# Last-visit chunk products of a gather-sum kernel: one float32 product becomes two float32r products

## The chip, the cores and the metric

The kernel runs on one NeuronCore of a Trainium2 chip. The metric is the device time of one execution in microseconds (us). The engines are TensorE (PE; PEld is its weight load), VectorE (DVE), ScalarE (ACT), GpSimd (POOL) and SyncE (SP, which issues DMAs).

## What is computed

The reference sums the features of 206,250 edges by their source node, puts the sums through a three-layer network with the node's own row, and normalises the result:

```python
edge_aggr = jnp.zeros((n, 128)).at[src].add(edge_attr_128)
combined = concatenate([x, edge_aggr, global_expand], axis=-1) @ W_c + b_c
h = softplus(combined @ W1 + b1)
h = softplus(h @ W2 + b2)
return layernorm(x + (h @ W3 + b3))
```

There are n = 6,250 nodes, and each row has 128 float32 values.

## The kernel before

The nodes are cut into 32 buckets of 196 (`BL`). The edge rows are read, sorted within a column of 122 by TensorE (line 1156), copied out of PSUM by ScalarE (line 1168) and scattered by 846 indirect DMAs of GpSimd (line 1185) into *rooms* of their bucket in the DRAM tensor `rows_by`. Once a stretch of a room is sure to be full, SP loads up to eight chunks of 128 rows back (a *load*, tile `chunks`, `AHEAD` = 6 of them in turn). A *visit* is a set of such chunks of one pair of buckets; a *unit* is at most four chunks of a load (`HALF`).

For each unit `match` (line 974) lets VectorE write one-hot tiles `hot` of 128 x 196 per chunk (line 985: is the row's place in its bucket equal to the column?), and `product` (line 993) multiplies each chunk's 128 x 128 rows with its one-hot tile on TensorE and accumulates in the PSUM tile `part` (line 1008). When a visit is complete, `add` (line 1017) lets VectorE add `part` into `sums_t` (line 1031). The last visits of all rooms have `col == NC`: they can be loaded only when every scatter has landed.

What is left of these steps when the sorting is over is the list `rest`, and `node_layers` (line 1337) weaves it into the network. There are 13 node tiles of up to 512 nodes. For a tile TensorE forms z of layer 1 (lines 1347 and 1348, the second needs the tile's sums), ScalarE runs three activations (1358, 1359, 1364), VectorE makes h (1372), TensorE forms z of layer 2 (1351), ScalarE and VectorE follow again, TensorE makes the last product (1386), and VectorE adds the node rows and takes the statistics (1394, 1397, 1401). `norm` (line 1405) runs for groups of three node tiles: a few small operations on VectorE and ScalarE give the factors `rs`, and then GpSimd normalises 12 blocks of 128 nodes (line 1428) and issues three output DMAs (line 1431). In the last two groups other engines do it or share it. GpSimd also adds the bias b3 to all node rows beforehand (line 1447).

The order on TensorE, VectorE, ScalarE and SP is the order in which the code is written out (`manual_schedule`), and GpSimd keeps the order of the program too. In `rest` the match of a unit is written four units ahead of its product (`AT_END`). An engine takes its instructions strictly in that order, so that one that waits holds up all behind it.

Of the kernel before, what the change touches and what calls it, by code (L numbers as in the profile page):

```python
# [6 lines left out]

F32 = mybir.dt.float32
BF16 = mybir.dt.bfloat16
F16 = mybir.dt.float16  # L10
I32 = mybir.dt.int32
# [3 lines left out]
ALU = mybir.AluOpType  # L15
# [3 lines left out]
P = 128  # L19

BL = 196
# [36 lines left out]
HALF = 4  # L58
# [15 lines left out]
SPAN = 48  # L74

SUMS = 2

ROWS = 4
BANKS = 3
# [63 lines left out]
def kernel(  # L143
# [21 lines left out]
    nc = tc.nc  # L165
    N, D = n_nodes, x.shape[2]
# [5 lines left out]
    NC = 2 * TB  # L172
# [67 lines left out]

    plain = const.tile(list(plain_in.shape), F32, name="plain")
    half = const.tile(list(half_in.shape), BF16, name="half")

# [11 lines left out]
    ident_h, wide_h = (of_half[n] for n in ("ident", "wide"))  # L255
    ones = const.tile([P, P], F32, name="ones")
    ones_h = const.tile([P, P], BF16, name="ones_h")
    zero_c = const.tile([P, ROW - W], F32, name="zero_c")
    sums_t = const.tile([P, NB * BL], F32, name="sums_t")
    most_of = const.tile([KB, 6 * G], F32, name="most_of")  # L260
    many_i = const.tile([1, 1], I32, name="many_i")
    c_bias = const.tile([P, 1], F32, name="c_bias")
    weights_sb = const.tile(list(weights_in.shape), F32, name="weights_sb")
# [13 lines left out]
    rows_by = dram.tile([ROWS_ALL, ROW], F32, name="rows_by")  # L277
    totals = dram.tile([N + 2, D], F32, name="totals")

    put = {"todo": []}  # L280

    def rows_dma(out, in_):
        for _ in range(2):
# [22 lines left out]
    hots = ctx.enter_context(tc.tile_pool(name="hots", bufs=6))  # L306
# [8 lines left out]
    with ExitStack() as phase:  # L315
# [15 lines left out]
        pair_i = src_i[:PN]  # L331
        pair_block = keep.tile([PN, NC], BF16, name="pair_block")
        pair_low = pair_i.bitcast(F32)
# [113 lines left out]
        def positions(g):  # L447
# [18 lines left out]
            def opened2():  # L466
                slot_of[g] = per.tile([P, 2 * B_MAX], F32, name="slot", bufs=3)
                pair_of[g] = per.tile([P, B_MAX], I32, name="pair", bufs=3)

            def opened():  # L470
                if sets:
                    if not split:
                        opened2()
                    own["odd"] = per.tile([KB, 2, Q_MAX], BF16, name="odd", bufs=1)
                    own["evens"] = per.tile([KB, Q_MAX], BF16, name="evens", bufs=1)
                    own["alone"] = per.tile([KB, Q_MAX], BF16, name="alone", bufs=1)
                    late, deep = ("_late", G - GAP) if split else ("", 1)
# [403 lines left out]
        def sum_steps():  # L881

            def form(item):
                of, b, c = item
                return (0, b) if not of else (THREE, 0) if of == THREE else (1 + (c >= CUT), 0)

            loads, units_of, in_visit = [], [], {}
            for v, (col, order, b0, b1, all_of) in enumerate(visits()):
# [18 lines left out]
                for of in mine:  # L907
                    if not of:
                        continue
                    n = -(-len(of) // HALF)  # L910
# [5 lines left out]
            for n, (j, _, _) in enumerate(units_of):  # L916
                last_unit[j] = n
            base_of = {v: min(bs) for v, bs in in_visit.items()}
            chunks, hots_of, parts_of, met, begun = {}, {}, {}, {}, set()
            awaits = [0]  # L920

            def load(j):
# [43 lines left out]
            def place_in(j, q):  # L966
                all_of = loads[j][3]
                of, _, c = all_of[q]
                if of in (0, THREE):
                    return q  # L970
                mixed = [x for x, item in enumerate(all_of) if form(item) == form(all_of[q])]
                return mixed[0] + 2 * (c - all_of[mixed[0]][2]) + of - 1

            def match(n):
                j, a, e = units_of[n]
                hot = hots.tile([P, HALF, BL], F32, name="hot")
                hots_of[n] = hot
                q = a
                while q < e:
                    lo = hi = place_in(j, q)  # L980
                    step, m = 1, 1
                    while q + m < e and place_in(j, q + m) > hi and (m == 1 or place_in(j, q + m) == hi + step):
                        step, hi = place_in(j, q + m) - hi, place_in(j, q + m)
                        m += 1
                    nc.vector.tensor_tensor(  # L985
                        hot[:, q - a:q - a + m],
                        chunks[j][:, lo:hi + 1:step, D:W].to_broadcast([P, m, BL]),
                        iota_ps.unsqueeze(1).to_broadcast([P, m, BL]), op=ALU.is_equal)
                    q += m
# [3 lines left out]
            def product(n):  # L993
                j, a, e = units_of[n]
                v, col, order, all_of = loads[j]
                t, hot = chunks[j], hots_of.pop(n)
                if v not in parts_of:
                    while len(pending) > SUMS - 1:
                        add()
                    parts_of[v] = ps.tile([P, 2, BL], F32, name="part", bufs=SUMS)  # L1000
                    met[v] = []
                part = parts_of[v]
                for q in range(a, e):
                    b = all_of[q][1]
                    first = b not in met[v]
                    met[v].append(b)
                    last = met[v].count(b) == in_visit[v].count(b)
                    nc.tensor.matmul(part[:, b - base_of[v], :], t[:, place_in(j, q), :D], hot[:, q - a],  # L1008
                                     start=first, stop=last)
                if n == last_unit[j]:  # L1010
                    del chunks[j]
                if len(met[v]) == len(in_visit[v]):
                    pending.append((v, order, col, n))
                if pending and n >= pending[0][3] + BEHIND:
                    add()

            def add():
                v, order, col, _ = pending.pop(0)
                part = parts_of.pop(v)
                got = sorted(set(met.pop(v)))  # L1020
                new = [b for b in got if b not in begun]
                begun.update(new)
                for bs, to in ((new, True), ([b for b in got if b not in new], False)):
                    if not bs:
                        continue
                    here = sums_t[:, bs[0] * BL:(bs[-1] + 1) * BL]
                    of = part[:, bs[0] - base_of[v]:bs[-1] - base_of[v] + 1].rearrange("p b n -> p (b n)")
                    if to:
                        nc.vector.tensor_copy(here, of)
                    else:  # L1030
                        nc.vector.tensor_add(here, here, of)  # L1031
                if col == NC:
                    summed["to"] = (NB if got[-1] == NB - 1 else got[-1]) * BL
# [3 lines left out]
            for n, (j, a, e) in enumerate(units_of):  # L1037
                while opened < j or (opened + 1 < len(loads) and opened + 1 <= j + AHEAD - 1
                                     and opened + 1 - AHEAD in freed):
                    opened += 1  # L1040
                    ready = FIRST + SCATTER * (loads[opened][1] // 2) + LAG
                    load_at[opened] = max(ready, freed.get(opened - AHEAD, 0.0))
                    found.append((load_at[opened], len(found), lambda j=opened: load(j)))
                    if opened < AHEAD:
                        freed.setdefault(opened - AHEAD, 0.0)
                ahead = AT_END if at > ends[-1] else TOGETHER
                match_at.append(max(load_at[j] + MATCHED, product_at[n - ahead] if n >= ahead else 0.0))
                product_at[n] = max(at, match_at[n] + MULTIPLIED)
                found.append((match_at[n], len(found), lambda n=n: match(n)))
                found.append((product_at[n], len(found), lambda n=n: product(n)))  # L1050
                at = product_at[n] + (e - a) * RATE
                if n == last_unit[j]:
                    freed[j] = product_at[n]
# [143 lines left out]
        with tc.manual_schedule(engines={ET.PE, ET.DVE, ET.Activation, ET.SP}):  # L1197
            by_part = src.rearrange("(p t) -> p t", p=P)

            def src_cols(a, b):  # L1200
# [7 lines left out]
                name=nc.get_next_instruction_name(), act_func_set_id=TABLES))  # L1208
# [89 lines left out]
            for g in range(G):  # L1298
# [9 lines left out]
                if NODES[0] <= g < NODES[1]:  # L1308
                    upto = len(nodes)
                    part = nodes[held:upto]  # L1310
# [6 lines left out]
            todo = fill_rows()  # L1317
# [13 lines left out]

    ahead = ctx.enter_context(tc.tile_pool(name="ahead", bufs=1))
    work = ctx.enter_context(tc.tile_pool(name="work", bufs=1))

    many = nc.values_load(many_i[:1, :1], min_val=0, max_val=6 * G * KB)

# [148 lines left out]
    with tc.If(many > 0):  # L1485
# [4 lines left out]
        for a in range(0, N + 2, P):  # L1490
            b = min(N + 2, a + P)
            nc.sync.dma_start(totals[a:b, :], zeros[:b - a])
        with tc.For_i(0, runs // every, 1) as i:
            rows = slow.tile([P, W], F32, name="slow_rows")
            part = slow.tile([P, 1], I32, name="slow_part")
# [8 lines left out]
            v = nc.vector  # L1504
# [13 lines left out]
            for n, by in enumerate((wide_h, ident_h)):  # L1518
# [8 lines left out]
                             start=True, stop=True)  # L1527
# [78 lines left out]
```

## Time and profile before

| | |
|---|---|
| three runs | 1298.19, 1300.34, 1302.69 us, median 1300.34 us |
| the profiled execution | 1298.19 us, its span 1296.3 us |
| mean granted TensorE clock | 0.966 |
| TensorE, VectorE, ScalarE, GpSimd busy | 1167.5, 1073.0, 1063.7, 877.4 us |

The span is what lies between the first and the last instruction; 1.89 us of the execution lie around it. In a row of a group, "busy" is the time that the group occupied the engine, and the mean is the length of one instruction; on TensorE instructions overlap, so that the pace of a stream is read from the distance of its starts. "idle before" names what ended the engine's wait. A float32 product stands as two MATMUL records, since it goes through TensorE in two passes, each with its own weight load.

### The profile page before, as it was taken

What the parts mean: (1) busy time and instruction counts of PE and PEld (TensorE: products, weight loads), DVE (VectorE), ACT (ScalarE), POOL (GpSimd) and SP (SyncE); (2) the same over time, 40 slices, a digit from 0 to 9 for tenths busy, and PEclk for the clock granted to TensorE, in tenths of its full rate; (3) what the DMA queues carried; (4) which work ended last, traced back from release to release, by engine and by line L of the source; (5) the groups of instructions that cost most, each with busy time, mean ns of one, the idle gap of its engine ahead of it and who ended that gap; (6) DMA issues with size and microseconds to landing.
All of it is one profiled execution on the core that took longest, in us unless ns stands there. A gap on an engine that the chain in (4) does not pass through costs nothing.

```text
span 1296.3 us, 26649 instructions
## 1 busy us (share of the span) xinstructions
PE 1167.5 (90%) x8617; PEld 1106.5 (85%) x8617; DVE 1073.0 (83%) x2403; ACT 1063.7 (82%) x2484; POOL 877.4 (68%) x915
## 2 busy tenths in 40 slices
PE   5767898878999898999899999999999999999893
PEld 4667788877998898998799999999999999898762
DVE  7968987998899988899878887799877766687784
ACT  5998998899987898987999999998999999504353
POOL 2777777777775677776777777777777777730334
PEclk9988998989999899999999999999999999999996
DMA  6789998899999999997989999999999999874421
GB/s 228 245 292 369 335 342 291 303 319 377 335 364 299 354 381 355 355 312 244 313 291 303 331 333 318 355 313 320 326 354 328 370 332 355 280 210 143 143 76 53
DMA packets 228719, 387.21 MB, mean 299 GB/s; under 512 B 27914, under 2 KB 139218, under 8 KB 228190
## 3 DMA queue, kind: packets, MB, share of 16 engines
q1 hardware_dynamic: 184831, 265.91, 63.1%
q0 software_dynamic: 41328, 115.65, 23.1%
q10 hardware_dynamic: 2415, 3.87, 0.8%
q8 instruction: 72, 1.18, 0.4%
q14 instruction: 73, 0.60, 0.1%
HBM read 242.49 MB, written 147.41 MB: 301 GB/s over the span
## 4 chain that ended last, share of the span: by engine, by line
PE 47%; DVE 18%; DMA 11%; ACT 8%; issue 8%; POOL 7%; SPq 0%; ACTq 0%; DVEq 0%; POOLq 0%
PE part L1008 27%; PE sorted L1156 14%; DMA rows_by<-pairs,pair 8%; POOL rows_by L1185 7%; ACT pairs L1168 5%; DVE hot L985 4%; DMA chunks<-rows_by 2%; ACT sort_hot L1143 2%; DVE sort_hot L1136 2%; DVE pair_ib L493 2%; DVE past L722 2%; DVE sums_t L1031 1%; DVE slot L571 1%; PE small L552 1%; PE small L554 1%
## 5 line engine op out<-in xcount | busy, mean ns | idle before, releaser
L1185 POOL DMA_INDIRECT rows_by<-pairs,pair x846 | 825.0, 975 | 305.2 <-issue 208.0
L1008 PE MATMUL part<-hot,chunks 128*128 128x196 f32 x3516 | 674.6, 335 | 12.8 <-DVE sums_t L1031 9.9
L1168 ACT COPY pairs<-sorted 64x387 f32<-64x387 f32 (+2 forms) x1144 | 542.6, 474 | 82.3 <-PE sorted L1156 62.7
L1008 PEld LDWEIGHTS part<-hot,chunks 128*128 128x128 f32 x3516 | 581.1, 193 | 22.0 <-DVE sums_t L1031 11.3
L1156 PE MATMUL sorted<-rows,sort_hot 122*128 122x129 f32 x3384 | 495.8, 287 | 44.4 <-ACT pairs L1168 35.4
L1156 PEld LDWEIGHTS sorted<-rows,sort_hot 122*128 122x128 f32 x3384 | 453.1, 198 | 55.9 <-ACT pairs L1168 52.8
L985 DVE TENSOR_TENSOR hot<-chunks,both_ps 128x784 f32<-128x784 f32 (+3 forms) x541 | 428.1, 810 | 5.4 <-DMA chunks<-rows_by 5.0
L1143 ACT ACTIVATE sort_hot<-plain,slot 122x128 f32<-122x128 f32 x846 | 278.3, 391 | 12.6 <-DVE slot L571 6.7
L1031 DVE TENSOR_TENSOR sums_t<-sums_t,part 128x392 f32<-128x392 f32 (+1 forms) x262 | 143.5, 548 | 118.0 <-PE part L1008 117.4
L1145 ACT ACTIVATE sort_hot<-sort_hot,ones 122x384 f32<-122x384 f32 (+2 forms) x286 | 174.6, 611 | 9.3
L1136 DVE TENSOR_TENSOR sort_hot<-slot,both_ps 122x384 f32<-122x384 f32 (+2 forms) x286 | 154.5, 541 | 3.2 <-PE sorted L1156 3.0
L493 DVE TENSOR_TENSOR pair_ib<-pair_block,both_ps 122x512 bf16<-122x512 bf16 (+2 forms) x157 | 103.5, 664 | 0.3
L1428 POOL TENSOR_SCALAR y<-y,mv,rs 128x128 f32<-128x128 f32 x40 | 31.1, 785 | 98.8 <-issue 69.5
L571 DVE TENSOR_REDUCE slot<-small 122x16 f32<-122x512 f32 (+2 forms) x109 | 72.8, 668 | 15.1 <-PE small L554 15.0
L1358 ACT ACTIVATE away<-sorted,z_bias 128x512 f32<-128x512 f32 (+2 forms) x13 | 8.5, 656 | 71.7 <-DMA chunks<-rows_by 47.1
L552 PE MATMUL small<-pair_ib,half 122*122 122x512 bf16 (+2 forms) x109 | 43.1, 395 | 10.1 <-DVE slot L571 9.8
L737 PEld LDWEIGHTS <-past 128*128 128x128 f16 x424 | 24.8, 99 | 18.7 <-DVE past L722 13.5
L722 DVE TENSOR_TENSOR past<-both_ps,starts 128x512 f16<-128x512 f32 (+1 forms) x61 | 39.9, 666 | 0.2
L737 PE MATMUL small<-jump,past 128*128 128x56 f16 (+3 forms) x424 | 29.2, 190 | 11.9 <-DVE past L722 8.8
L554 PEld LDWEIGHTS <-starts_h 128*122 128x122 bf16 x236 | 25.0, 147 | 12.2 <-issue 7.8
L722 DVE TENSOR_TENSOR past<-both_ps,starts_late 128x512 f16<-128x512 f32 (+2 forms) x49 | 32.3, 660 | 0.0
L504 PE MATMUL small<-ones_h,pair_ib 122*128 122x48 bf16 x423 | 18.0, 188 | 14.8 <-DVE pair_ib L493 14.7
(163 smaller groups left out, 523.6 us busy)
## 6 DMA issues: line engine op xcount, KB each, us to landing
rows<-in_edge SPq DMA_DIRECT2D x105, 1032.0 KB
chunks<-rows_by SPq DMA_DIRECT2D x362, 136.0 KB
chunks<-rows_by SPq DMA_DIRECT2D x203, 204.0 KB
chunks<-rows_by SPq DMA_DIRECT2D x75, 272.0 KB
rows_by<-pairs,pair POOLq DMA_INDIRECT x846
rows_by<-fill SPq DMA_DIRECT2D x21, 544.0 KB
rows_by<-fill SPq DMA_DIRECT2D x14, 816.0 KB
chunks<-rows_by SPq DMA_DIRECT2D x13, 408.0 KB
```

Of the source, the lines that this page charges most:

```text
L493: nc.vector.tensor_tensor(ib, pair_block[:, cols].unsqueeze(2).to_broadcast([PN, n, SB]), iota_ps[:PN, :SB].unsqueeze(1).to_broadcast([PN, ...
L571: nc.vector.tensor_reduce(to, of, axis=mybir.AxisListType.X, op=ALU.max)
L722: nc.vector.tensor_tensor(past[:, :, a:b], twice_ps[:KB].unsqueeze(1).unsqueeze(1).to_broadcast([KB, 2, b - a, P // 2]), own["starts"][:, ...
L985: nc.vector.tensor_tensor(hot[:, q - a:q - a + m], chunks[j][:, lo:hi + 1:step, D:W].to_broadcast([P, m, BL]), iota_ps.unsqueeze(1).to_bro ...
L1008: nc.tensor.matmul(part[:, b - base_of[v], :], t[:, place_in(j, q), :D], hot[:, q - a], start=first, stop=last)
L1031: nc.vector.tensor_add(here, here, of)
L1136: nc.vector.tensor_tensor(hot[:PN, :m], slot[:PN, at:at + 2 * m - 1:2].unsqueeze(2).to_broadcast([PN, m, P]), slot_ps[:PN].unsqueeze(1).to ...
L1143: nc.scalar.activation(hot[:PN, j], by_slot[:PN], AF.Abs, bias=slot[:PN, at:at + 1], scale=-1.0)
L1145: nc.scalar.activation(hot[:PN, :m], hot[:PN, :m], AF.Relu, bias=ones[:PN, :1], scale=-1.0)
L1156: nc.tensor.matmul(out[:, j, :], hot[:PN, j], rows_at[col // LOAD_COLS][:PN, col % LOAD_COLS, :], start=True, stop=True)
L1168: nc.scalar.copy(sets_at[i][64 * n:64 * n + 64, lo:lo + m, h, :W], out[64 * h:64 * h + 64, :m, :])
L1185: s = nc.gpsimd.indirect_dma_start(out=dst, out_offset=bass.IndirectOffsetOnAxis(ap=at, axis=0), in_=rows[:, j].rearrange("p a b -> p (a b ...
```

## The change

For units of the last visits (`fine`), each run of chunks in `match` is split before the one-hot is made: ScalarE copies the rows into a float32r tile `high` (which rounds them), GpSimd subtracts it from the rows and writes the remainder as the float32r tile `low`, and the one-hot tile is float32r as well. In `product` each chunk then has two products, `high` and `low`, in place of one of float32. The two new tiles have six buffers each. Other units keep the float32 product; their one-hot is the same bits read as float32.

```diff
+HALVES_AHEAD = 6
...
-                hot = hots.tile([P, HALF, BL], F32, name="hot")
+                hot = hots.tile([P, HALF, BL], F32R, name="hot")
+                fine = loads[j][1] == NC
+                if fine:
+                    part_of[n] = [late["pool"].tile([P, HALF, D], F32R, name=f"{name}_of", bufs=HALVES_AHEAD)
+                                  for name in ("high", "low")]
+                else:
+                    hot = hot.bitcast(F32)
...
+                    if fine:
+                        whole = chunks[j][:, lo:hi + 1:step, :D]
+                        high, low = (part[:, q - a:q - a + m] for part in part_of[n])
+                        nc.scalar.copy(high, whole)
+                        nc.gpsimd.tensor_tensor(low, whole, high.bitcast(F32), op=ALU.subtract)
                     nc.vector.tensor_tensor(
                         hot[:, q - a:q - a + m],
...
-                    nc.tensor.matmul(part[:, b - base_of[v], :], t[:, place_in(j, q), :D], hot[:, q - a],
-                                     start=first, stop=last)
+                    rows = [p[:, q - a] for p in part_of[n]] if n in part_of else [t[:, place_in(j, q), :D]]
+                    for k, of in enumerate(rows):
+                        nc.tensor.matmul(part[:, b - base_of[v], :], of, hot[:, q - a],
+                                         start=first and k == 0, stop=last and k == len(rows) - 1)
```

By the order of the program 196 chunks in 56 units are changed, with 66 copies on ScalarE and 66 subtractions on GpSimd: 32 of each over four chunks (128x512), 32 over two (128x256), one over three and one over one. VectorE's and SP's order is as before. Line numbers after the change are 15 or 16 higher from `match` on.

On TensorE, where the sorting has ended: before, 101 float32 products of chunks run up to the first node tile's z (in this listing a float32 product is one row).

```order
L1008 MATMUL part<-hot,chunks 128x196 x19
L1282 MATMUL small<-most_of,ones 1x48
L1008 MATMUL part<-hot,chunks 128x196 x101
L1347 MATMUL sorted<-x_t,fold 128x512
L1348 MATMUL sorted<-sums_t,fold 128x512
```

After, 72 of the 101 are still float32, and from the 73rd on each chunk is a pair of products, one from `high_of` and one from `low_of`.

```order
L1023 MATMUL part<-hot,chunks 128x196 x19
L1297 MATMUL small<-most_of,ones 1x48
L1023 MATMUL part<-hot,chunks 128x196 x72
L1023 MATMUL part<-hot,high_of 128x196
L1023 MATMUL part<-hot,low_of 128x196
L1023 MATMUL part<-hot,high_of 128x196
```

So 29 changed chunks stand ahead of the first z, and the other 167 between the node tiles.

On GpSimd, at the first group of node tiles: before, the bias additions to the node rows are followed at once by the first normalisation (y is the output block, mv and rs its statistics).

```order
L1447 TENSOR_TENSOR x_sb<-x_sb,b_all 128x256
L1447 TENSOR_TENSOR x_sb<-x_sb,b_all 114x128
L1428 TENSOR_SCALAR y<-y,mv,rs 128x128 x5
L1431 DMA out<-y 128x512
L1428 TENSOR_SCALAR y<-y,mv,rs 128x128 x4
L1431 DMA out<-y 128x512
L1428 TENSOR_SCALAR y<-y,mv,rs 128x128 x3
L1431 DMA out<-y 128x512
```

After, 45 subtractions stand ahead of that normalisation (these are the last of them), and the 46th and all later ones stand behind its 12 blocks.

```order
L997 TENSOR_TENSOR low_of<-chunks,high_of 128x256 x2
L997 TENSOR_TENSOR low_of<-chunks,high_of 128x512
L1444 TENSOR_SCALAR y<-y,mv,rs 128x128 x5
L1447 DMA out<-y 128x512
L1444 TENSOR_SCALAR y<-y,mv,rs 128x128 x4
L1447 DMA out<-y 128x512
L1444 TENSOR_SCALAR y<-y,mv,rs 128x128 x3
L997 TENSOR_TENSOR low_of<-chunks,high_of 128x512
L1447 DMA out<-y 128x512
L997 TENSOR_TENSOR low_of<-chunks,high_of 128x256 x2
```

The second normalisation stands in the same way between the 58th and the 59th subtraction. The 45 cover 129 chunks, the 13 between the two normalisations 42, and the last 8 cover 25.

On ScalarE, in the weave of the node tiles: before, the activations of two layers follow one another (away is the softplus's second part).

```order
L1358 ACTIVATE away<-sorted,z_bias 128x512
L1359 ACTIVATE away<-away 128x512
L1364 ACTIVATE away<-away,ones 128x512
L1358 ACTIVATE away<-sorted,b_c 128x512
L1359 ACTIVATE away<-away 128x512
L1364 ACTIVATE away<-away,ones 128x512
```

After, the copies of the coming units stand between these sixes.

```order
L996 CAST high_of<-chunks 128x256 x3
L996 CAST high_of<-chunks 128x512 x2
L1374 ACTIVATE away<-sorted,z_bias 128x512
L1375 ACTIVATE away<-away 128x512
L1380 ACTIVATE away<-away,ones 128x512
L1374 ACTIVATE away<-sorted,b_c 128x512
L1375 ACTIVATE away<-away 128x512
```

A copy thus follows the activations of a node tile, which wait for that tile's z.

More of the change, by code (lines that the diff above doesn't have):

```diff
@@ L8 @@
 F32 = mybir.dt.float32
+F32R = mybir.dt.float32r
 BF16 = mybir.dt.bfloat16
@@ L278 @@
     totals = dram.tile([N + 2, D], F32, name="totals")
-    put = {"todo": []}
+    put, late = {"todo": []}, {}
     def rows_dma(out, in_):
@@ L918, in sum_steps @@
             base_of = {v: min(bs) for v, bs in in_visit.items()}
-            chunks, hots_of, parts_of, met, begun = {}, {}, {}, {}, set()
+            chunks, hots_of, parts_of, part_of, met, begun = {}, {}, {}, {}, {}, set()
             awaits = [0]
@@ L1333 @@
     work = ctx.enter_context(tc.tile_pool(name="work", bufs=1))
+    late["pool"] = work
     many = nc.values_load(many_i[:1, :1], min_val=0, max_val=6 * G * KB)
```

## The prediction

> **What bounds the kernel now.** The change touches only the last visits, so I first find their stretch. The timeline of TensorE shows one run of 81 chunk products (162 records) up to the first node tile's z:
>
> ```profile
> 1136.40 28.71 PE L1008 MATMUL part<-hot,chunks 128*128 128x196 f32 x162 [3.34 <-DVE sums_t L1031]
> ...
> 1205.24 3.48 PE L1008 MATMUL part<-hot,chunks 128*128 128x196 f32 x20
> 1208.56 1.02 PE L1351 MATMUL sorted<-h,weights_sb 128*128 128x512 f32 x2
> 1209.42 1.05 PE L1386 MATMUL small<-weights_sb,h 128*128 128x128 f32 x8
> 1210.31 1.49 PE L1008 MATMUL part<-hot,chunks 128*128 128x196 f32 x8
> ...
> 1264.46 1.82 PE L1008 MATMUL part<-hot,chunks 128*128 128x196 f32 x10
> ```
>
> The last 29 of those 81 change; 104 records at 28.71/162 = 0.177 us put their start at 1154.8. The last row is the last chunk product, so the changed stretch is 1154.8 to 1266.3, 111.5 us. I cut it where the first two normalisations start on GpSimd:
>
> ```profile
> core 0: us, PE busy (x) PEld busy (x) DVE busy (x) ACT busy (x) POOL busy (x), PEclk, DMA share, GB/s
> 1154.80:1216.20 61.40, 58.15 (x304) 49.26 (x303) 48.18 (x100) 19.30 (x30) 0.00 (x0) 1.00 0.50 145
> 1216.20:1244.50 28.30, 25.74 (x132) 20.52 (x131) 23.25 (x59) 12.52 (x21) 11.12 (x15) 1.00 0.42 127
> 1244.50:1266.30 21.80, 20.46 (x105) 16.09 (x103) 17.37 (x48) 11.63 (x18) 11.04 (x15) 1.00 0.20 66
> ```
>
> TensorE is busy for 95, 91 and 94% of the three, DMA for at most half, ScalarE for 31 to 53%, GpSimd not at all or half. TensorE is the bound, but VectorE, with 78, 82 and 80%, is close behind: it has 13.2, 5.0 and 4.4 us to spare, and the change takes nothing off it. What VectorE waits for in the first and in the other two (the waits of that engine):
>
> ```profile
> DVE y L1394 <- PE small L1386: 7.0, 3, 2.6
> DVE sums_t L1031 <- PE part L1008: 2.8, 4, 1.3
> ...
> DVE y L1394 <- PE small L1386: 8.5, 6, 1.9
> ```
>
> So a faster TensorE can give at most 9.8 us in the first part and 8.5 in the other two, however fast it gets; then VectorE bounds.
>
> **The change, part by part.** *Products.* 196 chunks lose two float32 passes each. A pass costs (1208.56-1205.24)/20 = 0.166 us, together 392 x 0.166 = 65.1 us. In their place come 392 float32r products, a kind of which the trace has none. Its bounds: bf16 products, whose rows show 128 columns in (38.41-38.19)/4 = 0.055 us,
>
> ```profile
> 38.19 0.39 PE L554 MATMUL small<-half,starts_h 128*122 128x128 bf16 x4
> 38.41 0.44 PE L1156 MATMUL sorted<-rows,sort_hot 122*128 122x129 f32 x2
> ```
>
> give 196/128 x 0.055 = 0.084 us for 196; if each float32r product took two float32 passes, it would be 0.332. Between these lies the weight load. 128 float32 columns load in 193 ns on average, one column in 80:
>
> ```profile
> L1008 PEld LDWEIGHTS part<-hot,chunks 128*128 128x128 f32 x3516 | 581.1, 193 | 22.0 <-DVE sums_t L1031 11.3 <-issue 6.2 <-DVE hot L985 1.3
> ...
> L1282 PEld LDWEIGHTS small<-most_of,ones 128*1 128x1 f32 x2 | 0.1, 80 | 0.2 <-issue 0.2
> ```
>
> The 127 columns between take 113 ns, and the eight passes of 128 columns above keep a pace of (1210.31-1209.42)/8 = 0.111 us. Every float32r product has its own four-byte weights, so I take 0.111: the load sets the pace. That is 43.5 us, 21.6 less on TensorE, of which 14.2 in the 129 chunks of the first part. The Trainium skill, "TensorE: Matmul & The Clock Gate", section "LDWEIGHTS (loading the stationary operand)", gives columns/1.2 ns, 107 ns for 128. By that the products would take 41.9 us. The trace's 113 agrees within 6%.
>
> *Copies and subtractions.* The nearest rows are those of the activations that read SBUF and of GpSimd's additions:
>
> ```profile
> L1359 ACT ACTIVATE away<-away 128x512 f32<-128x512 f32 x22 | 13.9, 630 | 0.7
> ...
> L1359 ACT ACTIVATE away<-away 128x248 f32<-128x248 f32 x2 | 0.8, 409 | 0.1
> ...
> L1447 POOL TENSOR_TENSOR x_sb<-x_sb,b_all 128x512 f32<-128x512 f32 x11 | 13.5, 1275 | 0.1
> L1447 POOL TENSOR_TENSOR x_sb<-x_sb,b_all 128x256 f32<-128x256 f32 x1 | 0.7, 718 | 0.0
> L1447 POOL TENSOR_TENSOR x_sb<-x_sb,b_all 128x128 f32<-128x128 f32 x1 | 0.4, 445 | 0.0
> ```
>
> ScalarE: 32 x 0.63 + 32 x 0.41 + 0.8 = 34 us on 43.4 of 111.5; it stays free enough, and a copy late by a node tile's six activations (about 4 us) is mostly covered by the four units of lead. GpSimd: 32 x 1.275 + 32 x 0.718 + 1.0 + 0.4 = 65.2 us. Of these 43.2 (19 x 1.275 + 25 x 0.718 + 1.0) lie in the first part, where it is idle for all 61.4: hidden there, so the first part gains VectorE's 9.8 us. More than 13.2 (all its slack) it can't; if the copies come late, some 7.
>
> *The normalisations.* These are the heart of it. The timeline of GpSimd:
>
> ```profile
> 1216.47 3.90 POOL L1428 TENSOR_SCALAR y<-y,mv,rs 128x128 f32<-128x128 f32 x5 [69.49 <-issue]
> 1220.33 0.65 POOL L1431 DMA_DIRECT2D out<-y  x1
> 1221.03 3.11 POOL L1428 TENSOR_SCALAR y<-y,mv,rs 128x128 f32<-128x128 f32 x4
> 1224.09 0.62 POOL L1431 DMA_DIRECT2D out<-y  x1
> 1224.76 2.34 POOL L1428 TENSOR_SCALAR y<-y,mv,rs 128x128 f32<-128x128 f32 x3
> 1227.39 0.60 POOL L1431 DMA_DIRECT2D out<-y  x1 [0.30 <-POOL y L1428]
> 1244.73 3.88 POOL L1428 TENSOR_SCALAR y<-y,mv,rs 128x128 f32<-128x128 f32 x5 [16.74 <-DVE rs L1416]
> ...
> 1255.56 0.60 POOL L1431 DMA_DIRECT2D out<-y  x1 [0.30 <-POOL y L1428]
> ```
>
> A normalisation with its output DMAs holds GpSimd from 1216.47 to 1227.99, 11.5 us, the second as long. Nobody waited for that before. Now the 46th subtraction is queued behind the first, the 59th behind the second, and behind each missing `low` wait its unit's products, all later work of TensorE, then VectorE's adds. What covers it: four units whose match is written ahead, 196/56 = 3.5 chunks each, 4 x 3.5 x 0.222 = 3.1 us, and a z of layer 2 between, (1209.42-1208.56) = 0.86. Each stall is about 11.5-4.0 = 7.5 us. TensorE's clock drops after such a pause; the granted clock and the row of 1136.40 above show that a pause of 3.34 us was followed by
>
> ```profile
> 1136.00:1138.00 2.00, 1.60 (x5) 1.60 (x6) 2.00 (x4) 0.00 (x0) 2.00 (x3) 0.56 0.72 224
> 1138.00:1140.00 2.00, 2.00 (x9) 2.00 (x8) 1.14 (x2) 0.00 (x0) 2.00 (x2) 0.59 0.84 231
> ```
>
> that is 2 x 0.44 + 2 x 0.41 = 1.7 us of lost work. Part of that hides, since GpSimd then feeds only 56/65.2 units per us; I take 1.0, between 0 and 1.7. Each normalisation costs +8.5.
>
> *The other two parts.* Between the normalisations GpSimd has 16.74 us and must subtract 8 x 1.275 + 5 x 0.718 = 13.8: at most 2.9 us can be gained, I take 1.6. The last 25 chunks: TensorE saves 25 x 0.11 = 2.8, VectorE's waits allow less; 1.0.
>
> *Sum:* -9.8 + 8.5 - 1.6 + 8.5 - 1.0 = **+4.6 us**. The profiled execution would go from 1298.19 (span 1296.3 and 1.89 around it) to 1302.8; it was 2.15 below the median of the runs, so the median goes from 1300.34 to **1304.9 us**. About 0.3%, 3.9 us, is what a measurement of this kernel can tell from no change. With the ends (first part -13 to -7, stalls 6 to 9 with the clock, other parts -4 to 0 together) this case spans 1295 to 1311.
>
> **The rivals.**
> *Stalls hidden, faster.* If `low` runs far enough ahead, only the gains remain: -9.8-1.6-1.0 = -12.4, **1287.9 us**. The six buffers speak for it: six units and the z cover 6 x 0.78 + 0.86 = 5.5 us. Against it: the match is written only four units ahead, and 5.5 is not 11.5. The sign turns where a normalisation costs under 12.4/2 = 6.2 us. Chance 0.14.
> *Products at the bf16 pace, no change.* At 0.084 TensorE saves another 392 x 0.027 = 10.6 us, but VectorE takes up most: the first part ends at -11.5, the others 1.7 better together: +1.2, **1301.5 us**. The weight row of 113 ns speaks against it. A rule of the Trainium skill, "TensorE: Matmul & The Clock Gate", section "Weight-path perf modes — Fast Weight Load (FWL) and DoubleRow", says that 128 weights of a type other than FP32 load faster. Whether float32r counts as such the page doesn't say; with it the load would hide, as in this rival. No float32r load is in the trace. Chance 0.20.
> *A float32r product costs a float32 pass.* Then TensorE saves nothing. Four units now cover 4 x 1.16 = 4.6 us, a stall is 11.5-4.6-0.9 = 6.0, with the whole clock loss 7.7: +15.4, **1315.7 us**. For it: both have four-byte operands of 196 columns. Chance 0.14.
> *Two passes each.* 392 x 0.166 = 65 us more on a TensorE that is already the bound, with the stalls covered: **1365 us**. Then the split would be pointless; 0.06.
> If the copy to float32r kept all bits, `low` would be zero; that changes no time.
>
> **How the numbers follow.** The forecast has the remaining 0.46, of which 0.16 lies within 0.3%. Faster: 0.14 and 0.02 of the second rival, 0.16. Same: 0.16 + 0.17 = 0.33. Slower: 0.30 + 0.01 + 0.14 + 0.06 = 0.51. The range leaves out the rivals at 1288 and 1365, 0.20 together, and holds the others, 1315.7 with 2 us above it and the forecast's case but for its last us: 1296 to 1318.
>
> **What would show it.** Right: a float32r pace near 0.111 us; the first normalisation starting some 10 us earlier; TensorE idle for 6 to 9 us at each of the first two, released by GpSimd's subtraction, with a clock near 0.5 behind it; subtractions of 1.27 and 0.72 us. Wrong: no long wait of TensorE for GpSimd; a pace of 0.166 or more; a first part that gains over 13 us, which would mean that VectorE was not its limit.

## The result, and the profile after

The changed kernel takes **1304.39 us** (median of 20 runs, 1301.63 to 1307.99) where the kernel before takes 1298.37 (median of 20, 1294.03 to 1302.69): a ratio of 1.0042, 95% interval 1.0031 to 1.0054. It is slower, by some 5 to 6 us. The profiled execution took 1306.39 us (span 1304.6), that of before 1298.19 (span 1296.3).

To see where the 8.3 us between the two spans arise, I cut both tails at the same events: the first product of a changed chunk, then the start of VectorE's last row for the scale of a normalisation (its last `rs` row of 12 columns; GpSimd can start some 0.3 us later), for the three normalisations on GpSimd, then the end. In the kernel before, the first cut is the product in the same place, the 58th record ahead of the first node tile's z (29 chunks of two records). The windows of before, with the busy time of each engine, the granted clock and the DMA share:

```profile
core 0: us, PE busy (x) PEld busy (x) DVE busy (x) ACT busy (x) POOL busy (x), PEclk, DMA share, GB/s
1155.33:1216.12 60.79, 57.54 (x299) 48.65 (x299) 47.57 (x100) 19.22 (x30) 0.00 (x0) 1.00 0.50 144
1216.12:1244.45 28.33, 25.77 (x132) 20.55 (x131) 23.28 (x59) 12.54 (x21) 11.12 (x15) 1.00 0.42 127
1244.45:1268.07 23.62, 22.19 (x115) 17.34 (x114) 18.54 (x52) 12.52 (x22) 11.04 (x15) 1.00 0.18 61
1268.07:1296.30 28.23, 6.81 (x30) 4.51 (x28) 12.54 (x53) 10.93 (x25) 14.16 (x19) 0.64 0.18 61
```

And those of the changed kernel:

```profile
1155.46:1210.67 55.21, 48.69 (x305) 38.51 (x303) 47.06 (x100) 35.56 (x71) 37.23 (x40) 0.94 0.57 171
1210.67:1246.26 35.59, 24.08 (x132) 18.13 (x130) 23.35 (x58) 18.31 (x35) 24.50 (x28) 0.86 0.32 99
1246.26:1276.64 30.38, 22.39 (x110) 16.66 (x109) 18.62 (x51) 16.03 (x30) 18.99 (x23) 0.83 0.07 27
1276.64:1304.60 27.96, 7.54 (x30) 4.98 (x28) 12.34 (x53) 10.94 (x25) 14.19 (x19) 0.62 0.18 61
```

The first part is 5.6 us shorter, the second 7.3 and the third 6.8 longer, the rest 0.3 shorter. With the start 0.1 later that is the 8.3. In the second and third parts TensorE is no longer busy for 91 to 94% of the time but for 68 and 74%, and its clock, whole before, is at 0.86 and 0.83. What it waits for there, from its timeline:

```profile
1222.86 0.53 PE L1023 MATMUL part<-hot,low_of 128*128 128x196 f32 x1 [6.60 <-POOL low_of L997]
...
1258.36 0.53 PE L1023 MATMUL part<-hot,low_of 128*128 128x196 f32 x1 [5.32 <-POOL low_of L997]
```

These two waits, the longest of the two parts, are for one subtraction each. Why those came late is in the chain of waits, followed back from the first of them (start, length, what):

```profile
1210.67 0.18 DVE rs L1432
1210.85 0.10 issue
1210.94 0.80 POOL y L1444
1211.74 0.00 issue
1211.74 3.11 POOL y L1444 x4
1214.85 0.60 POOL out L1447
1215.45 0.05 issue
1215.51 2.79 POOL y L1444 x4
1218.29 0.28 issue
1218.57 0.62 POOL out L1447
1219.19 0.05 issue
1219.23 2.34 POOL y L1444 x3
1221.57 1.24 POOL low_of L997
1222.81 0.04 issue
1222.86 3.31 PE part L1023 x14
```

From 1210.94 to 1221.55 GpSimd does nothing but twelve blocks of the normalisation and two of its three output DMAs; the subtraction, 1.24 us long, stands behind them. TensorE follows 0.05 us after it.

The groups of the new work (form, count, busy time, mean ns of one, and the idle time ahead of them):

```profile
L997 POOL TENSOR_TENSOR low_of<-chunks,high_of 128x512 fp32r<-128x512 f32 x32 | 40.3, 1278 | 16.6 <-ACT high_of L996 16.6
L997 POOL TENSOR_TENSOR low_of<-chunks,high_of 128x256 fp32r<-128x256 f32 x32 | 22.8, 733 | 7.6 <-ACT high_of L996 7.5
L996 ACT CAST high_of<-chunks 128x512 fp32r<-128x512 f32 x32 | 19.0, 614 | 15.8 <-POOL low_of L997 12.1 <-DMA chunks<-rows_by 3.5
L996 ACT CAST high_of<-chunks 128x256 fp32r<-128x256 f32 x32 | 11.6, 400 | 5.8 <-DMA chunks<-rows_by 2.4 <-issue 1.7 <-PE part L1023 1.6
```

The start of the changed products in TensorE's timeline (start, length):

```profile
1155.68 0.28 PE L1023 MATMUL part<-hot,low_of 128*128 128x196 f32 x1
1155.80 0.28 PE L1023 MATMUL part<-hot,high_of 128*128 128x196 f32 x1
...
1156.24 0.28 PE L1023 MATMUL part<-hot,high_of 128*128 128x196 f32 x1
```

A subtraction takes 1278 or 733 ns, a copy 614 or 400. From 1155.68 to 1156.24 are five steps from product to product (three rows in between are left out here). Matmuls overlap, so the pace is read from the starts and not from the lengths: (1156.24-1155.68)/5 = 0.112 us.

### The profile page after: what moved, and what is told of

The parts are those of the page before. It is cut to its first block, busy times and chain, and to the rows that moved or that the text cites. A ratio compares the mean times of both kernels' runs of the same rounds, so it can differ in the third digit from the quotient of the medians.

```text
span 1304.6 us, 26906 instructions
## 1 busy us (share of the span) xinstructions
PE 1156.9 (89%) x8617; PEld 1093.6 (84%) x8617; DVE 1071.1 (82%) x2403; ACT 1092.3 (84%) x2550; POOL 941.0 (72%) x981
## 4 chain that ended last, share of the span: by engine, by line
PE 46%; DVE 17%; DMA 13%; ACT 10%; POOL 7%; issue 6%; ACTq 0%; SPq 0%; DVEq 0%; POOLq 0%
PE part L1023 25%; PE sorted L1171 15%; DMA rows_by<-pairs,pair 9%; ACT pairs L1183 6%; POOL rows_by L1200 5%; DVE hot L998 3%; DMA chunks<-rows_by 3%; ACT sort_hot L1158 2%; DVE past L724 2%; DVE sort_hot L1151 2%; DVE pair_ib L495 2%; POOL y L1444 1%; DVE slot L573 1%; DVE sums_t L1046 1%; PE small L554 1%
## 5 line engine op out<-in xcount | busy, mean ns | idle before, releaser
L1023 PE MATMUL part<-hot,chunks 128*128 128x196 f32 x3124 | 604.4, 335 | 8.3 <-DVE sums_t L1046 7.4
L1171 PE MATMUL sorted<-rows,sort_hot 122*128 122x129 f32 x3384 | 496.2, 286 | 44.8 <-ACT pairs L1183 35.6
L1023 PEld LDWEIGHTS part<-hot,chunks 128*128 128x128 f32 x3124 | 515.7, 193 | 10.1 <-DVE sums_t L1046 7.9
L998 DVE TENSOR_TENSOR hot<-chunks,both_ps 128x588 f32<-128x588 f32 (+5 forms) x541 | 426.9, 808 | 4.5 <-DMA chunks<-rows_by 4.2
L1158 ACT ACTIVATE sort_hot<-plain,slot 122x128 f32<-122x128 f32 x846 | 278.3, 391 | 12.4 <-DVE slot L573 6.5
L997 POOL TENSOR_TENSOR low_of<-chunks,high_of 128x512 fp32r<-128x512 f32 (+2 forms) x66 | 63.5, 997 | 26.5 <-ACT high_of L996 26.5
L996 ACT CAST high_of<-chunks 128x512 fp32r<-128x512 f32 (+2 forms) x66 | 29.8, 504 | 51.1 <-DVE hot L998 29.3
L1023 PE MATMUL part<-hot,high_of 128*128 128x196 f32 x196 | 54.9, 320 | 9.6 <-DVE sums_t L1046 8.3
L1023 PE MATMUL part<-hot,low_of 128*128 128x196 f32 x196 | 49.3, 291 | 11.9 <-POOL low_of L997 11.9
L1023 PEld LDWEIGHTS part<-hot,low_of 128*128 128x128 f32 x196 | 40.5, 207 | 15.4 <-POOL low_of L997 12.7
L1023 PEld LDWEIGHTS part<-hot,high_of 128*128 128x128 f32 x196 | 40.5, 207 | 14.1 <-ACT high_of L996 5.0
```

The lines of the kernel that those rows point to most:

```text
L997: nc.gpsimd.tensor_tensor(low, whole, high.bitcast(F32), op=ALU.subtract)
L998: nc.vector.tensor_tensor(hot[:, q - a:q - a + m], chunks[j][:, lo:hi + 1:step, D:W].to_broadcast([P, m, BL]), iota_ps.unsqueeze(1).to_bro ...
L1023: nc.tensor.matmul(part[:, b - base_of[v], :], of, hot[:, q - a], start=first and k == 0, stop=last and k == len(rows) - 1)
L1158: nc.scalar.activation(hot[:PN, j], by_slot[:PN], AF.Abs, bias=slot[:PN, at:at + 1], scale=-1.0)
L1171: nc.tensor.matmul(out[:, j, :], hot[:PN, j], rows_at[col // LOAD_COLS][:PN, col % LOAD_COLS, :], start=True, stop=True)
```

## The experiments

My theory: the twelve blocks of a normalisation, put ahead of a subtraction on GpSimd, stall TensorE at two places and cost more than the cheaper products bring. The rivals: the split's own work on ScalarE and GpSimd costs the time; the products are the trouble. Four of the runs, those with 1595.44 in the table's third column, come from a chip on which the kernel before takes that long; there I go by the ratio and by the parts of the tail, which agree with those of the other runs. GpSimd's order is set by a scheduler, which keeps to the program but for moves such as that of the third output DMA above; kernels that cut up a normalisation fix it to the order in which the code is written (`ET.Pool` is added to `manual_schedule`).

The parts as cut above, in us (where an expectation below names a third part of 27.8 us, it ends at the last chunk product and not at the third normalisation):

| kernel | time | kernel before beside it | ratio, 95% interval | first | second | third | rest |
|---|---|---|---|---|---|---|---|
| before (profile above) | | | | 60.8 | 28.3 | 23.6 | 28.2 |
| after (profile above) | 1304.39 | 1298.37 | 1.0031 to 1.0054 | 55.2 | 35.6 | 30.4 | 28.0 |
| after, again | 1303.73 | 1298.34 | 1.0029 to 1.0055 | 52.0 | 35.3 | 30.2 | 28.0 |
| both cut up, first run | 1586.21 | 1595.44 | 0.9916 to 0.9970 | 52.0 | 27.7 | 23.2 | 28.7 |
| both cut up, again | 1290.61 | 1298.34 | 0.9920 to 0.9952 | 53.6 | 28.2 | 23.6 | 28.6 |
| both cut up, lead of six | 1289.96 | 1298.34 | 0.9923 to 0.9949 | 52.2 | 27.3 | 23.4 | 28.7 |
| one cut up | 1300.19 | 1298.48 | 0.9995 to 1.0025 | 53.7 | 27.9 | 33.0 | 28.6 |
| as after, lead of six | 1299.69 (one run) | 1298.34 | | 52.2 | 31.3 | 28.8 | 27.9 |
| first part alone split | 1588.33 | 1595.44 | 0.9944 to 0.9992 | 55.2 | 28.0 | 23.6 | 28.0 |
| the same, again | 1292.92 | 1298.48 | 0.9940 to 0.9976 | 53.6 | 29.6 | 23.6 | 28.0 |
| float32 products | 1591.98 | 1595.44 | 0.9947 to 0.9994 | 60.8 | 29.1 | 23.9 | 28.3 |
| the same, again | 1300.12 | 1298.48 | 1.0006 to 1.0030 | 60.8 | 29.1 | 23.9 | 28.4 |
| high alone | 1578.53 | 1595.44 | 0.9876 to 0.9936 | 50.1 | 28.9 | 21.4 | 28.3 |
| lead of six, x products twice | 1295.91 | 1298.48 | 0.9972 to 0.9995 | 57.1 | 26.9 | 24.3 | 28.7 |

**Both normalisations cut up.** The blocks of the first two normalisations go into a list, and each subtraction is followed by one of them:

```
 nc.gpsimd.tensor_tensor(low, whole, high.bitcast(F32), op=ALU.subtract)
+if owed:
+    owed.pop(0)()
...
-    (nc.vector if last else nc.gpsimd).tensor_scalar(y[:r, q, :], ...)
+    owed.append(block)     # the same tensor_scalar; its tile's DMA behind the last block
...
-with tc.manual_schedule(engines={ET.PE, ET.DVE, ET.Activation, ET.SP}):
+with tc.manual_schedule(engines={ET.PE, ET.DVE, ET.Activation, ET.SP, ET.Pool}):
```

> The first two normalisations are cut up: GpSimd runs one block of 128x128 behind each subtraction, in the order in which they are written, instead of twelve in a row. All work stays. Stall theory (TensorE waits for a subtraction that is queued behind a whole normalisation): the waits of 6.60 and 5.32 us and the halved clock behind them go, the second and third parts come back from 35.6 and 27.8 us to some 27 and 21.5, and the time is 1289 to 1293 us, below both kernels. Rival (the split's own work on ScalarE and GpSimd, or the float32r products, cost the time): the order on GpSimd matters little, 1302 to 1306 us.

> The normalisations cut up between the subtractions, beside the changed kernel on the same chip. Stall theory: 0.989 to 0.995 of the kernel before, 10 to 15 us under the changed kernel, and no wait of TensorE for GpSimd over 1 us. Rival (the gain of the first run was the chip's spread): 0.998 to 1.006.

Ratio 0.9943 in the first run and 0.9936 in the second (1290.61 us, 13 us under the changed kernel beside it). GpSimd's timeline in the second run, at the place of the first stall:

```profile
1212.45 1.28 POOL L997 TENSOR_TENSOR low_of<-chunks,high_of 128x512 fp32r<-128x512 f32 x1 [2.68 <-ACT high_of L996]
1213.72 0.80 POOL L1453 TENSOR_SCALAR y<-y,mv,rs 128x128 f32<-128x128 f32 x1
1214.50 0.72 POOL L997 TENSOR_TENSOR low_of<-chunks,high_of 128x256 fp32r<-128x256 f32 x1
1215.21 0.78 POOL L1453 TENSOR_SCALAR y<-y,mv,rs 128x128 f32<-128x128 f32 x1
```

No wait of TensorE for GpSimd is left in that run, and the second and third parts are back at 28.2 and 23.6, those of before. The work of the changed kernel is all there, only its order differs: the stalls were the loss. The edit also fixes GpSimd's order as such; that this alone is not the cure shows in the run with one normalisation cut up, below, where the order is fixed too and the normalisation left in one piece still stalls TensorE.

**The changed kernel again.**

> The changed kernel itself once more, beside the kernel before on the same chip. Stall theory: 1.003 to 1.006 of the kernel before; the two waits of TensorE for a subtraction behind a normalisation come again, 6.6 and 5.3 us. The 2.2 us wait in the first part comes again too; if the clock halves behind it, the first part is 55 to 56 us long, if not (as in the first of these runs), 52. Rival (the chip of the first four runs hides the stalls, since all else is slower there): 0.998 or less.

The ratio came again (1.0042, 1.0029 to 1.0055) with waits of 5.18 and 5.32 us. The first wait is 1.4 us under the 6.60 that I expected, and yet the second part is as long (35.3 against 35.6): TensorE's clock was at 0.50 from 1213.8 to 1217.2 here, ahead of the wait, so that TensorE reached the missing chunk later. New was the first part, 52.0 us where the first profile had 55.2. I come back to it below.

**One normalisation cut up** (`if parts_at[0] in (0,)` in place of `(0, 1)`).

> Only the first of the two normalisations is cut up, the second stays in one piece. Stall theory, dose for dose: the first wait (5 to 7 us) is gone, the second (5.3 us) is there as before; second part 27 to 29 us, third part 30 us; half of the gain, 1296 to 1299 us where the kernel before takes 1298. Rival (one change of order on GpSimd sets everything behind it right, or the other way round): the time of both cut up, 1290, or of none, 1304.

The second part is cured (27.9), the third is not, dose for dose:

```profile
1252.79 0.53 PE L1025 MATMUL part<-hot,low_of 128*128 128x196 f32 x1 [7.09 <-POOL low_of L997]
```

That wait is 1.8 us longer than I expected, and so is the time (1300.19, a little over the expected end of 1299): with the order fixed, all three output DMAs stand ahead of the waiting subtraction and each waits 0.3 us for its last block, so that GpSimd is held for 12.1 us (1239.32 to 1251.46) and not for 10.5, as where the scheduler had let the third DMA slip behind the subtraction. The third part is 33.0 us where I expected 30; its clock is 0.79 against the 0.83 of the changed kernel.

**A longer lead**, in the changed kernel (`AT_END` 6 in place of 4) and in the one with both cut up.

> The changed kernel with the match written six units ahead in place of four, normalisations in one piece as they were. Stall theory, by the forecast's own working (a stall is the block on GpSimd less the lead): each wait at a normalisation is 2 x 0.78 = 1.6 us shorter, 5.0 and 3.7 us. Rival (the stall is not covered by the lead, since all buffers are full and the subtraction behind the block is the same one): 6.6 and 5.3 us as before.

> As the one before, with the match written six units ahead of the product in place of four. Theory (what is left in the first part is the 2.2 us wait for copies that stand behind a node tile's activations on ScalarE, and the clock behind it): the wait goes, the first part comes to 50 to 52 us whatever the clock did, 1 to 4 us under the kernel with four. Rival (VectorE is the limit there, as the forecast had it; or six buffers for six units leave none to spare, and copies wait for products): no gain, within 1 us, or a loss.

In the changed kernel the two waits are now

```profile
1222.05 0.36 PE L1023 MATMUL part<-hot,low_of 128*128 128x196 f32 x1 [3.84 <-POOL low_of L997]
...
1253.76 0.53 PE L1023 MATMUL part<-hot,low_of 128*128 128x196 f32 x1 [2.60 <-POOL low_of L997]
```

1.3 to 2.8 us shorter than those of the two profiles above: the lead works as cover, by about the 1.6 expected or more. (The time of this kernel is a single run; its waits and parts carry the reading.) For the kernel with both cut up my expectation fell. I had put the 2.2 us wait in the first part down to copies behind a node tile's activations on ScalarE. With two more units of lead it stands there unchanged:

```profile
1196.66 0.33 PE L1025 MATMUL part<-hot,high_of 128*128 128x196 f32 x1 [2.17 <-DVE sums_t L1048]
```

and the kernel is not faster beyond doubt (1289.96 against 1290.61). The releaser named in the row was right: VectorE's add. VectorE's timeline just ahead of that wait in the changed kernel shows what the add of 1194.27 is queued behind, the last layer's y and its statistics, with no gap from 1192.03 on:

```profile
1192.03 0.69 DVE L1410 TENSOR_TENSOR y<-small,x_sb 128x512 f32<-128x512 f32 x1 [0.77 <-PE small L1402]
1192.75 0.87 DVE L1413 BATCH_NORM_STATS2 stats<-y 128x6 f32<-128x128 f32 x4
1193.54 0.36 DVE L1417 BATCH_NORM_AGGREGATE mv<-stats 128x2 f32<-128x6 f32 x4
1193.82 0.53 DVE L998 TENSOR_TENSOR hot<-chunks,both_ps 128x392 fp32r<-128x392 f32 x1
1194.27 0.55 DVE L1046 TENSOR_TENSOR sums_t<-sums_t,part 128x392 f32<-128x392 f32 x1
```

**High alone** (the remainder is left out: no subtraction, one float32r product a chunk).

> The remainder is left out: no subtraction and one float32r product for each chunk (its output lacks the remainder's share). Stall theory: nothing on TensorE waits for GpSimd; with 0.111 us for a chunk in place of 0.222 TensorE stands well clear of the bound, and VectorE's work sets the three parts: 1279 to 1287 us. Rival (GpSimd is not what holds the changed kernel back, ScalarE's copies behind the activations are): the second and third parts stay above those of before, 1290 us or more.

The first part of its windows:

```profile
1440.56:1490.69 50.13, 38.01 (x183) 26.50 (x181) 46.81 (x100) 35.67 (x71) 0.00 (x0) 0.89 0.63 187
```

What TensorE waits for there (us in total, times, longest):

```profile
PE part L1021 <- DVE sums_t L1044: 7.3, 5, 2.6
PE sorted L1362 <- DVE sums_t L1044: 3.1, 2, 2.1
```

129 products of 0.111 us fewer, 14.3 us, and the part is only 1.9 us shorter than that of the changed kernel's second profile (52.0). VectorE is busy for 46.8 of 50.1 us, and TensorE waits for its adds: VectorE is the limit there. The ratio of 0.9906 is 15 us on that chip's 1595, the tail is 12.3 us shorter than that of before (141.0 to 128.7), within the 11 to 19 us expected.

**First part alone split** (`fine` only up to the 45th subtraction, those ahead of the first normalisation).

> Only the units of the first 45 subtractions, those ahead of the first normalisation, are split; the later chunks go in as plain float32, as before the change. Stall theory: the first part keeps its gain of about 6 us, the rest is as before the change, 1291 to 1294 us. Rival (copies and subtractions cost what the products save, wherever they stand): no gain, 1297 to 1300 us.

> Only the units of the first 45 subtractions are split, beside a kernel before that takes 1298 us. Stall theory: the first part gains 6 (with the clock halved behind its 2.2 us wait) to 9.5 us (without), the rest is that of before: 0.993 to 0.996 of the kernel before. Rival: no gain, 0.998 or more.

Faster both times, 0.9968 and 0.9958. The change as it stands gains where GpSimd has nothing else to do, and the 67 chunks that stay in float32 give up little (1292.92 against 1290.61 for all of them with the normalisations cut up).

**Float32 products** (copies and subtractions run, nothing reads them).

```
-rows = [p[:, q - a] for p in part_of[n]] if n in part_of else [t[:, place_in(j, q), :D]]
+rows = [t[:, place_in(j, q), :D]]
```

> ScalarE's copies and GpSimd's subtractions all run, but nothing reads them: the products take the chunks in float32 as before the change. Stall theory: the copies and subtractions lie beside other work, and a normalisation ahead of them keeps nobody waiting: the time of before, 1297 to 1301 us. Rival (the split's own work holds the activations, and through them the node layers): 1302 us or more.

> All copies and subtractions run and nothing reads them. Its first run came out at 0.997 of the kernel before, while the three parts in its trace were those of before. Theory (the work on ScalarE and GpSimd is hidden): 0.999 to 1.002, parts of 61, 29 and 24 us. Rival (the order of the tail's other work changed with it and gained 4 us): 0.997 again, and a part that is shorter than before by as much.

The two disagree in the whole time, 0.9971 and 1.0018, but not in the tail: 60.8, 29.1, 23.9 both times, the first part that of before, 0.3 to 0.8 us over before in the second and third part. I take the tail: the work on ScalarE and GpSimd costs at most some 2 us (1.0030 is 3.9 us at the far end). The 0.997 came from elsewhere in the program, on a chip where the runs of the kernel before lie 19 us apart; what it was is open.

**x products twice** (with both cut up and the lead of six: the layer-1 product that needs no sums is issued twice, 0.87 us more for TensorE in each node tile).

> The kernel with both normalisations cut up and six units of lead; each layer-1 product that needs no sums is made twice, so that TensorE has 0.87 us more to do in the pauses ahead of the sums. Theory (the clock is halved behind pauses that come close together): less half clock at the start of the second and third part, up to 2.5 us in each, where VectorE leaves room for 0.5 to 1: 0 to 2 us under 1290. Rival (the halving doesn't go by how much of a pause is filled, or VectorE, not the clock, sets the time there): no gain, 1290, or 1 to 3 us above, the price of the added products on TensorE.

The second part has its clock at 1.00 throughout (0.94 without) and is 0.4 us shorter, the third shows no change of the clock (0.93) and is 1.0 longer, and the first part, with six node tiles, is 57.1 us long in place of 52.2: the added products, and a clock of 0.97 in place of 1.00. The work cost 6 us, more than the rival had allowed. That it held the clock in the second part is not shown: the last section shows that such a pause halves the clock in some profiles and not in others of one and the same kernel.

## Why the prediction was right, step by step

The forecast was 1304.9 us and the time is 1304.39, by the mechanism that it named: the two stalls behind the normalisations cost more than the products gain. That the time came within 0.5 us is luck in part. The change was forecast as +4.6 us and is +6.0 (+5.4 beside the second before); the forecast stood on 1300.34, the median of three runs, and 20 runs gave 1298.37. And its terms did not all have their size.

- **Products: 0.111 us, right.** The pace is 0.112, and the rivals at 0.084, 0.166 and 0.332 are out. That the weight load sets this pace is argued and not shown: no run has float32r products of another width. The Trainium skill, "TensorE: Matmul & The Clock Gate", section "Weight-path perf modes — Fast Weight Load (FWL) and DoubleRow", says that 128 weights of a type other than FP32 load faster. Here float32r weights keep the pace of float32 ones, so the trace doesn't bear out that the rule reaches float32r.
- **Copies and subtractions: right.** 614, 400, 1278 and 733 ns against the 630, 409, 1275 and 718 of the rows that they were taken from.
- **First part: -9.8, "VectorE bounds", right in kind, and in size when the clock holds.** -8.8 in the second profile (52.0), -5.6 in the first (55.2), against 60.8 before. (The forecast put the start of before at 1154.8 by the mean pace of a run that begins at half clock; counted record by record it is 1155.33.) The 3.2 between the two is TensorE's clock, halved behind the 2.2 us wait in one and not in the other. The forecast had put no price on the clock here. *High alone* shows the limit to be VectorE.
- **A stall of 7.5 us and 1.0 of clock at each normalisation: +17.0, too large by 3.3.** The waits were 5.2 to 6.6 and 5.3. GpSimd was held for 10.6 us and not 11.5, since the third output DMA stands behind the subtraction, which the order listing ahead of the prediction already shows. The subtraction's own 1.24 us, which the forecast left out, comes on top. And TensorE came to rest only 5.3 to 6.7 us after the block's start, where the forecast took a cover of 4.0: 10.6+1.24-5.3 = 6.5 and 10.6+1.24-6.7 = 5.1. Against the kernel with both cut up the second and third parts lose 35.3-28.2 = 7.1 and 30.2-23.6 = 6.6 us, so 1.3 to 1.9 go beyond the waits, half clock behind them among it. +13.7 in place of +17.0.
- **Between and last: -1.6 and -1.0, too large as well.** Without stalls those two parts are 28.2 and 23.6, against 28.3 and 23.6 of before: -0.2 and 0.0.
- **Sum:** -8.8+13.7-0.2-0.3 (the rest) = +4.4 in the second profile, where +4.6 was forecast. That these agree is luck too: gains and stalls were both put too large, and the errors cancel. The medians lie 5.4 to 6.0 us apart. The difference of 1.0 to 1.6 is perhaps the clock in the first part, which halves in some profiles; the changed stretch also began later in every profile of a split kernel beside a before of 1298 than in the one profile of before (1155.46 and 1157.82 in the two of the changed kernel, against 1155.33). Whether that is chance is open.
- **The rival on the other side (stalls hidden, 1287.9)** has its outcome, not its way, in the cut-up kernel: 1290. The forecast's gains without stalls, -12.4, came out as -8.
- **Its signs.** The pace, the lengths of the subtractions and the half clock at the waits came as said. The waits were mostly shorter than the 6 to 9 us named, and the first normalisation started 5.7 and 8.9 us earlier, counted from the start of the changed stretch, in place of some 10.

## What to carry to other kernels

When work moves to an idle engine, don't ask how busy that engine is but what is queued ahead of each new instruction there: one block of 10.6 us at two places cost 13.7 us against 8.8 gained in the first part (second profile), on an engine that had been idle for most of the stretch. A long job without a deadline (a normalisation with its output) is cut up and dealt out between short jobs that another engine waits for. That made the same change 0.6% faster than the kernel before instead of 0.4% slower.

## What the hardware showed unexpectedly

**A pause of 2.2 us can halve TensorE's clock, or not.** The same wait in two profiles of the changed kernel, first in TensorE's timeline of the first profile:

```profile
1194.97 0.50 PE L1023 MATMUL part<-hot,high_of 128*128 128x196 f32 x1 [2.18 <-DVE sums_t L1046]
```

The windows behind it (length, busy times, granted clock, DMA share):

```profile
1195.00:1198.00 3.00, 3.00 (x10) 2.48 (x11) 3.00 (x6) 0.83 (x3) 3.00 (x3) 0.50 0.70 210
1198.00:1201.00 3.00, 3.00 (x7) 1.45 (x7) 2.26 (x4) 0.53 (x1) 1.48 (x3) 0.50 0.28 74
```

The timeline of the second profile:

```profile
1197.35 0.33 PE L1023 MATMUL part<-hot,high_of 128*128 128x196 f32 x1 [2.18 <-DVE sums_t L1046]
```

And its windows:

```profile
1197.50:1200.50 3.00, 3.00 (x17) 2.04 (x18) 3.00 (x6) 0.98 (x3) 3.00 (x4) 1.00 0.73 215
1200.50:1203.50 3.00, 3.00 (x24) 2.52 (x23) 2.62 (x5) 1.96 (x4) 1.40 (x3) 1.00 0.32 87
```

The wait is 2.18 us in both; the clock is 0.50 behind the first and 1.00 behind the second. It stayed halved for 6.8 us there (1194.75 to 1201.57) and for 3.4 in the second run of the kernel with both cut up (1198.1 to 1201.5). Every change of the granted clock in the first profile lies a whole number of steps of 3.41 us from the others, and what the pause does goes by how it lies on these steps. The step ahead of the halving in the first profile, then the two steps that share the pause in the second:

```profile
1191.34:1194.75 3.41, 1.45 (x14) 1.28 (x12) 2.69 (x12) 3.35 (x8) 1.20 (x2) 1.00 0.65 223
1193.29:1196.70 3.41, 1.88 (x17) 1.71 (x15) 2.60 (x12) 3.19 (x7) 0.84 (x3) 1.00 0.72 232
1196.70:1200.11 3.41, 2.76 (x13) 1.84 (x14) 3.41 (x8) 1.51 (x4) 3.41 (x4) 1.00 0.58 167
```

TensorE is busy for 1.45 us of the step that is followed by half clock, and for 1.88 and 2.76 of those that are not. Ten profiles have this pause: the clock halved in six, where the least busy step that it touches was busy for 0.36 to 0.47 of its length, and held in four, with 0.51 to 0.64. The edge is not sharp: a step with 1.77 of 3.41 us busy was followed by half clock in the run with both cut up and a lead of six (1209.67 to 1213.08), and by whole clock in that with x products twice (1208.20 to 1211.61). The Trainium skill, "TensorE: Matmul & The Clock Gate", section "What's actually happening", speaks of a window of about 3.4 us that runs freely and doesn't start anew with the kernel. The steps of 3.41 us, and the same pause with either outcome, agree with that. By the same section of the Trainium skill the clock goes down after an idle window. That the whole window has to be idle doesn't agree with the traces, since a pause of 2.2 us was enough.

**One chip differed by far more than the change.** The kernel before took 1595 us on one chip and 1298 on the others, while for the same kernel each part of the tail was the same to within 1.6 us. With *float32 products* the same 387 MB moved at 244 GB/s there and at 299 on another chip, over the whole span. Why, and whether it is the chip or how it stood at that time, wasn't tried.
